# New figures, an overlap, tie numbers and four rules in the planner of a metaformer layer on one core

## The chip, the cores and the metric

The kernel runs on one core of one Trainium2 chip. The metric is the device time of one execution in microseconds (us). Before the change it is 3187.56 us, the median of 3 runs (3181.11 to 3189.2).

## What is computed

One metaformer layer on x of shape (8, 384, 32, 32), all in float32: 8 images b, each 1024 tokens of 384 channels. First comes a selective state-space block with its own MLP, then a feed-forward block with sign-binarised weights and group-wise 8-bit quantisation. Cut to what matters:

```python
# block 1, tokens t = layernorm(x)
xz = t @ in_proj_w.T;  xm, z = split(xz)                  # 768 channels each
xc = silu(causal_conv3(xm))
dt, Bm, Cm = split(xc @ x_proj_w.T)                       # 24, 16, 16
dt = softplus(dt @ dt_proj_w.T + dt_proj_b)
h[l] = exp(dt[l] * A) * h[l-1] + (dt * xc)[l] * Bm[l]     # 16 states a channel, 1024 steps
y = (sum over states of h * Cm + xc * D) * silu(z)
x = x + gelu((y @ out_proj_w.T) @ mlp_w1.T + b1) @ mlp_w2.T + b2
# block 2, images 0 to 4 alone get a quantised branch that is not zero
h = quant(layernorm(x) @ sign(W1 - mean).T + b1)
x = x + quant(gelu(h) @ sign(W2 - mean).T + b2)
```

Quantisation needs the largest absolute value of a whole image, twice per image.

## The kernel before, in words

All work of the eight images is written down once as a list of operations and then put in order by a planner that runs while the program is built. `Layer.write_down` (L1286 on) goes through the images: `s1` (L654: norm, input projections, convolution, dt), `s2` and `scan` (L813, L826: the recurrence), `s3` (L1001: output projection and MLP) and, for images 0 to 4, `ffn` (the quantised block). Each `Plan.add` (L212) records an engine, a cost in us, a function that issues the instruction, and the tiles it reads and writes. From the tiles the planner derives which operation waits for which.

`Plan.run` (L258) is a list scheduler. It keeps a clock for each engine (`free`), takes the engine that can start first, lets `choose` (L281) pick one of the operations that can start at that moment (`able`, those whose start is not after `now`), issues it, and advances the engine's clock by the cost. So the costs decide the order of the instructions on each engine and nothing else; each engine then executes its list in that order. The parts that matter here:

- Engines. TensorE (PE) does all matrix products, and the sums over states of the scan (`py`, L907). GpSimd (POOL) does the products with B and C (`u`, `dtx_r`, L942). VectorE (DVE) does the scans (L967), a part of the C products (L987, L989), convolution taps and some copies out of PSUM. ScalarE (ACT) does the exponentials `da` (L556), the silu, softplus and gelu functions (L556 as well) and most copies out of PSUM (L569, L571). SP issues nearly all transfers.
- Choice on ACT. exp, silu, softplus and gelu need different function tables; a change costs an ACT_TABLE_LOAD (planner's price `LOAD_TABLE` 1.29). `choose` stays in the loaded table while such an operation can start (`same`, except exp), else takes an exp or an operation without a table (`plain`), and changes to another table only when neither can start.
- Groups of functions. `in_place` (L670) and `gelu` apply a function to three pieces of 128x1024. The first piece reads all parts of the group (`r=parts if p == 0`), and the second and third overwrite parts the first has read; so they depend on the first, and their `ready` time is its end (L378 on, with no signal added, since the engine is the same).
- Choice on DVE and POOL. Operations of the stages (`prio[0] > 0`) go before those of the scan (`prio[0] == 0`).
- Ties. `rank` (L295) orders by lane, image and age. In each 100 us of planned time, a number from `TURNS` scrambles the age by up to 16 places (`turned`, L96).
- Fillers. Where the planner sees PE idle for more than `IDLE` 0.7 us, it puts matmuls of a constant there (`spare`, 128x256, L443 to L454), to hold the TensorE clock up. They do no part of the computation.
- Buffers: two PSUM tiles for `da`, three for products (`mm`), one for `py`; three `u` and two `dtx_r` in SBUF, nine `hid` for the hidden layer.
- The end. After the last `py` come the last products of the last half image in a row: `p_out`, 36 `p_h`, 36 `p_o` and the last store.

Of the kernel before, what the change touches and what calls it, by code (L numbers as in the profile page):

```python
# [71 lines left out]
MM = 0.86  # L72
SWITCH = 0.26
BATCH = 2
# [12 lines left out]

STRETCH, REACH = 100, 16
TURNS = (
# [3 lines left out]
)  # L93


def turned(n, by):  # L96
# [3 lines left out]
    return (x ^ x >> 13) % (2 * REACH + 1) - REACH  # L100


def c_act(n):
    return 0.25 + n * 0.00084


def c_dve(n):
    return 0.19 + n * 0.00102


def c_pair(n):
    return 0.19 + n * 0.00188


def c_pool(n):
    return 0.18 + n * 0.00214

# [81 lines left out]
class Plan:  # L199
# [12 lines left out]
    def add(self, engine, cost, emit, r=(), w=(), claim=(), table=None, size=0, others=None,  # L212
            land=1.6):
        op = Op()
        op.engine, op.cost, op.emit, op.table = engine, cost, emit, table
        op.others, op.settle = others or {}, None
        op.size, op.land, op.prio = size, land, (*self.prio, len(self.ops))
        op.next, op.ready, op.tiles = [], 0.0, []
        op.slack = SLACK if self.prio[0] < 0 else 0.0
        deps = set()  # L220

        def parts_of(t):
            t, part = t if isinstance(t, tuple) else (t, None)
            if t not in op.tiles:
                op.tiles.append(t)
                if t.ring is not None:
                    t.left += 1
            if part is None:
                if None not in t.parts:
                    t.parts[None] = [None, []]  # L230
                return list(t.parts.values())
            if part not in t.parts:
                whole = t.parts.get(None)
                t.parts[part] = [whole[0], list(whole[1])] if whole else [None, []]
            return [t.parts[part]]

        for t in claim:
            t.left += 1
            op.tiles.append(t)
        for t in r:  # L240
            for p in parts_of(t):
                if p[0] is not None:
                    deps.add(p[0])
                p[1].append(op)
        for t in w:
            for p in parts_of(t):
                if p[0] is not None:
                    deps.add(p[0])
                deps.update(p[1])
                p[0], p[1] = op, []  # L250
        deps.discard(op)
        op.wants = len(deps)
        for d in deps:
            d.next.append(op)
        self.ops.append(op)
        return op

    def run(self):  # L258
# [22 lines left out]
        def choose(e, now, able):  # L281
            able = [op for s, op in able if s <= now]
            if e == "ACT":
                same = [op for op in able if op.table == table and table != "exp"]
                plain = [op for op in able if op.table in (None, "exp")]
                able = same if table is not None and same else plain or able
            if e in ("DVE", "POOL"):

                able = [op for op in able if op.prio[0] > 0 and op.ready <= now - PATIENCE] or [
                    op for op in able if op.prio[0] == 0] or able  # L290
            at = int(now / STRETCH)
            turn = TURNS[at] if at < len(TURNS) else 0
            return min(able, key=lambda op: rank(op, turn))

        def rank(op, turn):  # L295


            lane, b = op.prio[:2]
            if lane <= 0:
                first = (lane, b)  # L300
            elif lane == 7:
                first = (EARLY, b)
            elif lane in (1, 4, 11, 14):
                first = (1, b) if b <= max(scanned + 1, FRONTS) else (3, b)
            else:
                first = (2, b)
            return (*first, op.prio[2] + (turned(op.prio[2], turn) if turn else 0))

# [12 lines left out]
        while left:  # L321
# [45 lines left out]
            if op.table is not None and op.table != table:  # L367
                cost += LOAD_TABLE
                table = op.table
            end = free[e] = clock.run(now, cost) if e == "PE" else now + cost  # L370
            if e == "SP":
                dma_free = max(dma_free, end + 0.5) + 0.05 + op.size / 360e3
                end = dma_free + op.land
# [17 lines left out]
class Layer:  # L391
# [115 lines left out]

    def load(self, to, view, src, r=(), size=0, cost=0.46, land=2.3):

        self.plan.add(  # L510
            "SP", cost, lambda: self.nc.sync.dma_start(view(to.real), src), r=r, w=[to],
            size=size, land=land,
        )
# [8 lines left out]
    def rows_moved(self, t, parts, move, r, w):  # L522
        n = P // len(parts)
        for i, mem in enumerate(parts):
            self.plan.add(
                "SP", 0.42, lambda i=i, mem=mem: move(t.real[i * n : (i + 1) * n, :], mem),
                r=r, w=w(i), size=4 * n * T,
            )

    def weights(self, ring, k, src, r=()):  # L530
        w = self.piece(ring, [P, k, P], ring)
        self.load(w, lambda t: t, src, r=r, size=4 * P * k * P, cost=0.37, land=1.5)
        return w
# [28 lines left out]
    def affine(self, out, in_, r, w, bias=0.0, scale=1.0, n=T, pool=False):  # L562
# [19 lines left out]
        if pool:  # L582
            others = {"POOL": (0.18 + n * 0.00095, on(nc.gpsimd))}
        else:
            others = {"DVE": (c_dve(n), on(nc.vector))}
        extra = 0.0 if plain else 0.09 if isinstance(scale, float) else 0.18
        self.plan.add("ACT", 0.16 + n * 0.00083 + extra, on_act, r=r, w=w, others=others)

    def norm(self, t, eps, scale):

        nc, add = self.nc, self.plan.add
        def columns(src, name):
# [10 lines left out]

            add("PE", 0.9, emit, r=[src], w=[p])
            return p

        def spread(src, name, turned=False):
# [29 lines left out]
        p_turned = self.piece("mm", [P, G], "p_turned")  # L637
        add("PE", 0.5, lambda: nc.tensor.matmul(
            p_turned.real, var.real, self.ident[:, ::DQ], start=True, stop=True
# [3 lines left out]
            r=[p_turned], w=[rstd])  # L643
        add("POOL", 0.8, lambda: nc.gpsimd.tensor_tensor(
            rstd.real, rstd.real, self.power.to_broadcast([P, G]), ALU.pow
# [8 lines left out]
    def s1(self, b):  # L654
# [46 lines left out]
        for half, cols in enumerate(HALVES):  # L701
# [4 lines left out]
            for m in range(KD):  # L706
# [12 lines left out]
                for s in (1, 2):  # L719
                    add("DVE", c_dve(T) + 0.06, lambda m=m, xc=xc, pm=pm, s=s, tap=tap: (  # L720
                        nc.vector.scalar_tensor_tensor(
# [4 lines left out]
            if half:  # L726
# [6 lines left out]

                add("POOL", 0.9, edge, r=[halo[m] for m in range(KD)], w=[self.edged])
                for p, piece in enumerate(xc.pieces):
                    add("POOL", 0.25, lambda p=p, piece=piece: nc.gpsimd.tensor_add(
                        piece.real[:, :, :2], piece.real[:, :, :2],
# [19 lines left out]

            add("PE", 0.26 + KC * MM, low, r=[w, *all_m], w=[p_dbc], claim=[dbc])
            self.affine(lambda dbc=dbc: dbc.real, lambda p_dbc=p_dbc: p_dbc.real, [p_dbc], [dbc])
# [66 lines left out]
    def scan(self, b, half, state):  # L826
# [7 lines left out]

        def load(to, view, src, r, size):
            self.plan.add("SP", 0.57, lambda: nc.sync.dma_start(view(), src), r=r, w=[to],  # L836
                          size=size, land=2.3)

        def quad_rows(i):
            r = self.piece(f"bc{i}", [P, n], f"bc{i}")  # L840
            src = rows.real[i * SQ : (i + 1) * SQ, cols].unsqueeze(0).to_broadcast([DQ, SQ, n])
            load(r, lambda: r.real, src, [rows[h] for h in halves], 4 * P * n)
            return r
# [90 lines left out]
    def scan_pair(self, u, cols, n, dts, dtxs, bq, cq, state, half, on_pool):  # L934
# [14 lines left out]
        for t, mine in enumerate(cols):  # L949
            da = self.piece("da", [P, wide, n], "da")  # L950
            dt_r = dts[t]
            for i, col in enumerate(mine):
                self.act(
                    lambda i=i, da=da: da.real[:, i, :],
                    lambda i=i, dt_r=dt_r: dt_r.real[:, i, :], AF.Exp,
                    0.26 + n * 0.00084, r=[dt_r[i]], w=[da], table="exp",
                    scale=self.a_neg[:, col : col + 1],
# [43 lines left out]
    def s3(self, b):  # L1001
        nc, a, add = self.nc, self.a, self.plan.add
        yg_d = self.dram["yg", b]
        for half, cols in enumerate(HALVES):
# [12 lines left out]
            else:  # L1017
                yg = self.split("hid", KD, "yg")
                for p, piece in enumerate(yg.pieces):
# [5 lines left out]
                        w=[piece[k] for k in range(PER)], claim=yg.pieces[p:],  # L1025
                        size=4 * P * PER * T, land=2.3,
                    )
# [21 lines left out]
            for m in range(KC):  # L1049
                rows = slice(m * P, (m + 1) * P)  # L1050
                res = self.piece("res", [P, T], "res")

                self.load(res, lambda t: t, a["x"][b, rows, cols], r=[g[HK]], size=4 * P * T)
                po = self.mlp_out(lambda i, m=m: a["mlp_w2"][m, i], "w6", g, [res], "p_o")
# [145 lines left out]
    def clip(self, view, n, parts, q):  # L1200
        self.plan.add("POOL", 0.13 + n * 0.0009, lambda: self.nc.gpsimd.tensor_scalar(
            view(), view(), q.real[:, 2:3], q.real[:, 1:2], ALU.min, ALU.max
        ), r=[q], w=parts)

    def ffn(self, b):
# [32 lines left out]
        for h, cols in enumerate(HALVES):  # L1238
            g = self.split("hid", KH, "gf")
            for p, piece in enumerate(g.pieces):  # L1240
# [3 lines left out]
                    r=[y1_d[h, p * PER + m] for m in range(PER)], w=parts,  # L1244
                    claim=g.pieces[p:], size=4 * P * PER * T, land=2.3)
                self.clip(lambda piece=piece: piece.real, PER * T, parts, q1)
# [135 lines left out]
```

## Time and profile before

| What | Value |
|---|---|
| Median of 3 runs | 3187.56 us |
| Profiled execution | 3184.62 us, its span 3182.5 us, mean TensorE clock 0.988 |
| Instructions in the trace | 33759 |
| Matmul records | 10972, two for each float32 matmul |
| Mean DMA rate | 236 GB/s, 751.85 MB |

An engine's busy time is the union of its instructions' times. A matmul of the program leaves two records, so a record count is twice the number of matmuls. Idle time of an engine is put down to what ended it ("<- ACT da L556" is an activation that writes `da`). The chain that ended last starts at 2928.10 us and is made mostly of PE in its last 100 us.

### The profile page before, as it was taken

The page shows a single profiled execution, that of the slowest core. Times are in us where ns is not written, and L with a number is a line of the kernel's source. Part 1 is how long each engine was busy: PE and PEld are TensorE (multiplying, and loading weights), DVE is VectorE, ACT ScalarE, POOL GpSimd, SP SyncE. Part 2 cuts the span into 40 slices and gives each one's busy share as a digit, 9 for nine tenths or more (in the row PEclk, how much of TensorE's full clock was granted, in tenths as well). Part 3 has the DMA queues.
Part 4 walks back from the last instruction along what each step waited for, and adds up shares of the span by engine and source line. Part 5 has one row for each costly group of instructions (what it writes and reads, how often), then busy time and mean ns, then how long its engine had stood idle before and what let it go on. Part 6 is the DMA issues. An engine that isn't in the chain of part 4 may idle for free. (4 is left out here: it accounts for less than half of the span.)

```text
span 3182.5 us, 33759 instructions
## 1 busy us (share of the span) xinstructions
PE 3083.4 (97%) x10972; PEld 1274.9 (40%) x10972; DVE 2644.0 (83%) x2081; ACT 1966.5 (62%) x2363; POOL 2744.8 (86%) x1046
## 2 busy tenths in 40 slices
PE   9898999999999999999999999999999999999999
PEld 4333434343433443433444434343434443433334
DVE  4697888899788798879998888889789987888881
ACT  4777786855665556665656655666566555655552
POOL 1788889988988978999979999799989999998980
PEclk9998999999989999999999999999999999999999
DMA  7797789757786667875696766877677856756542
GB/s 231 261 310 263 252 261 329 255 195 259 239 283 221 198 227 254 295 250 185 230 319 234 252 207 232 298 236 254 219 257 254 282 196 213 235 175 209 160 148 72
DMA packets 348975, 751.85 MB, mean 236 GB/s; under 512 B 36481, under 2 KB 113793, under 8 KB 339585
## 3 DMA queue, kind: packets, MB, share of 16 engines
q1 hardware_dynamic: 348368, 749.61, 71.0%
q8 instruction: 88, 1.44, 0.2%
q14 instruction: 87, 0.70, 0.1%
q10 hardware_dynamic: 432, 0.09, 0.0%
HBM read 569.21 MB, written 180.36 MB: 236 GB/s over the span
## 5 line engine op out<-in xcount | busy, mean ns | idle before, releaser
L942 POOL TENSOR_TENSOR u<-dtx_r,bc 128x2048 f32<-128x2048 f32 (+1 forms) x360 | 1185.5, 3308 | 124.9 <-PE py L907 79.7
L556 ACT ACTIVATE da<-dt_r,a_neg 128x1024 f32<-128x1024 f32 (+1 forms) x960 | 900.5, 945 | 490.0 <-DVE u L967 272.3
L942 POOL TENSOR_TENSOR u<-u,bc 128x2048 f32<-128x2048 f32 (+1 forms) x274 | 900.1, 3290 | 86.9 <-DVE u L967 81.4
L967 DVE TENSOR_TENSOR_SCAN u<-da,u 128x1024 f32<-128x1024 f32 (+1 forms) x436 | 869.1, 2007 | 127.1 <-POOL u L942 71.4
L540 PE MATMUL p_h<-t,w_b 128*128 128x512 f32 x1152 | 511.7, 597 | 10.8 <-DMA w_b<-in_mlp_w 6.8
L540 PE MATMUL p_o<-g,w 128*128 128x512 f32 x1152 | 512.6, 597 | 5.1 <-DMA w<-in_mlp_w 5.1
L967 DVE TENSOR_TENSOR_SCAN da<-da,dtx_r 128x1024 f32<-128x1024 f32 (+1 forms) x192 | 386.3, 2019 | 55.6 <-POOL dtx_r L942 34.2
L942 POOL TENSOR_TENSOR dtx_r<-dtx_r,bc 128x2048 f32<-128x2048 f32 (+1 forms) x120 | 396.8, 3311 | 2.4
L540 PEld LDWEIGHTS p_h<-t,w_b 128*128 128x128 f32 x1152 | 214.0, 190 | 298.0 <-issue 257.7
L540 PEld LDWEIGHTS p_o<-g,w 128*128 128x128 f32 x1152 | 214.3, 190 | 295.8 <-issue 277.9
L540 PE MATMUL p_y<-tn,w_b 128*128 128x512 f32 x720 | 319.6, 597 | 2.2 <-DVE tn L648 2.2
L540 PE MATMUL p_y<-gf,w_n 128*128 128x512 f32 x720 | 320.3, 597 | 0.8 <-ACT gf L556 0.5
L907 PE MATMUL py<-u,fold 128*32 128x512 f32 x2304 | 303.5, 628 | 0.2 <-POOL u L942 0.2
L967 DVE TENSOR_TENSOR_SCAN da<-da,u 128x1024 f32<-128x1024 f32 (+1 forms) x140 | 283.7, 2041 | 13.7 <-POOL u L942 6.9
L540 PE MATMUL p_out<-yg,w 128*128 128x512 f32 x552 | 245.6, 597 | 4.2 <-DMA w<-in_out_proj_last 1.5
L540 PE MATMUL p_z<-t,w_f 128*128 128x512 f32 x504 | 233.4, 610 | 9.2 <-DMA w_f<-in_in_proj_w 5.1
L540 PE MATMUL p_in<-t,w_f 128*128 128x512 f32 x504 | 229.7, 601 | 5.6 <-DMA w_f<-in_in_proj_w 3.7
L556 ACT ACT_TABLE_LOAD x172 | 220.7, 1283 | 3.1
L540 PEld LDWEIGHTS p_y<-gf,w_n 128*128 128x128 f32 x720 | 133.9, 190 | 185.3 <-issue 173.8
L540 PEld LDWEIGHTS p_y<-tn,w_b 128*128 128x128 f32 x720 | 134.0, 190 | 182.1 <-issue 165.1
L571 ACT ACTIVATE g<-p_h,v_vecs 128x512 f32<-128x512 f32 x158 | 107.7, 684 | 145.2 <-PE p_h L540 144.7
L571 ACT ACTIVATE y<-p_y,v_vecs 128x512 f32<-128x512 f32 x138 | 94.2, 684 | 166.9 <-PE p_y L540 139.0
(132 smaller groups left out, 3245.0 us busy)
## 6 DMA issues: line engine op xcount, KB each, us to landing
dt_r<-dt_d SPq DMA_DIRECT2D x144, 512.0 KB, 5.5
dtx_r<-dtx_d SPq DMA_DIRECT2D x72, 1024.0 KB, 6.0
w_b<-in_mlp_w SPq DMA_DIRECT2D x192, 192.0 KB, 3.1
w<-in_mlp_w SPq DMA_DIRECT2D x96, 384.0 KB, 3.5
w_f<-in_in_proj_w SPq DMA_DIRECT2D x168, 192.0 KB, 4.8
y_d<-y SPq DMA_DIRECT2D x120, 256.0 KB, 4.7
gf<-y_d SPq DMA_DIRECT2D x60, 512.0 KB, 6.9
xc_d<-xc SPq DMA_DIRECT2D x48, 512.0 KB, 5.6
```

The costliest lines, as they stand in the source:

```text
L540: self.nc.tensor.matmul(p.real, w.real[:, w0 + k, :], t.at(k0 + k), start=start and k == 0, stop=stop and k == n - 1,)
L556: lambda: self.nc.scalar.activation(out(), in_(), func, **{k: v() if callable(v) else v for k, v in kw.items()}),
L571: nc.scalar.activation(out(), in_(), AF.Identity, bias=bias, scale=scale)
L907: nc.tensor.matmul(py.real[g * DQ : (g + 1) * DQ, :], self.fold, hc, start=False, stop=(q == NQUAD - 1), skip_group_check=True,)
L942: nc.gpsimd.tensor_mul(u.real[:, x], t.real[:, x], row.real.unsqueeze(2).to_broadcast([P, n, 2]))
L967: da=da, in_u=in_u: nc.vector.tensor_tensor_scan(to(i), da.real[:, i, :], in_u(i), state.real[:, col : col + 1] if half else 0.0, ALU.mult ...
```

## The change

No operation of the computation is added or removed, and no buffer changes; what changes is what the planner believes and how it chooses.

1. Overlap (`LAG`): the planner's clock of ACT runs free 0.09 us before the operation's end, that of DVE 0.08 us before.
2. Figures: base costs of ACT, DVE and POOL operations, of several PE operations, and the rates and landing times of transfers. A transfer now occupies the planned DMA queue for 0.03 us plus its size by its own rate, and every landing gets 0.2 us more.
3. A new table `TURNS` of 29 numbers for 100 us each. Its lower 16 bits are the tie number as before. Four bits above switch rules on in that stretch: `LATE_FRONTS` (the front stage of a next image ranks behind the other stages), `DVE_SCANS` and `POOL_SCANS` (the scan goes before the stages on that engine), `ACT_STAGES` (among operations of ACT without another table, those of the stages go first). `LATE_FRONTS` stands in 7 stretches, `DVE_SCANS` in 5, `POOL_SCANS` in 6, `ACT_STAGES` in 6.

The diff, without lines that change one figure of the same kind:

```diff
-SWITCH = 0.26
+SWITCH = 0.22
...
+LATE_FRONTS, DVE_SCANS, POOL_SCANS, ACT_STAGES = 1 << 16, 1 << 17, 1 << 18, 1 << 19
 TURNS = (
-    19522, 59978, 49910, 0, 34827, 0, 6565, 14275, 0, 7565, 33371, 19911,
-    57895, 25116, 28986, 13399, 22123, 50761, 24784, 16788, 35300, 27386, 48162, 5457,
-    0, 0, 40719, 11435, 20253, 0, 2806, 25936,
+    55348, 285972, 34779, 0, 32856, 50975, 5477, 811041, 712524, 58073,
+    309902, 321043, 90863, 34708, 35186, 643484, 561450, 159751, 20316, 55659,
+    17295, 33505, 202442, 110152, 635446, 91750, 507399, 59652, 924931,
 )
...
+LAG = {"ACT": 0.09, "DVE": 0.08}
...
 def c_act(n):
-    return 0.25 + n * 0.00084
+    return 0.2 + n * 0.00084
 def c_dve(n):
-    return 0.19 + n * 0.00102
+    return 0.17 + n * 0.00102
 def c_pair(n):
-    return 0.19 + n * 0.00188
+    return 0.22 + n * 0.00188
...
     def add(self, engine, cost, emit, r=(), w=(), claim=(), table=None, size=0, others=None,
-            land=1.6):
+            land=1.6, rate=350e3):
...
-        op.size, op.land, op.prio = size, land, (*self.prio, len(self.ops))
+        op.size, op.land, op.prio = 0.03 + size / rate, land + 0.2, (*self.prio, len(self.ops))
...
         def choose(e, now, able):
             able = [op for s, op in able if s <= now]
+            at = int(now / STRETCH)
+            turn = TURNS[at] if at < len(TURNS) else 0
             if e == "ACT":
                 same = [op for op in able if op.table == table and table != "exp"]
                 plain = [op for op in able if op.table in (None, "exp")]
                 able = same if table is not None and same else plain or able
+                if turn & ACT_STAGES:
+                    able = [op for op in able if op.prio[0] > 0 and op.table in (None, "exp")] or able
             if e in ("DVE", "POOL"):
-                able = [op for op in able if op.prio[0] > 0 and op.ready <= now - PATIENCE] or [
-                    op for op in able if op.prio[0] == 0] or able
-            at = int(now / STRETCH)
-            turn = TURNS[at] if at < len(TURNS) else 0
+                scans = [op for op in able if op.prio[0] == 0]
+                if not (turn & (DVE_SCANS if e == "DVE" else POOL_SCANS) and scans):
+                    able = [op for op in able if (
+                        op.prio[0] > 0 and op.ready <= now - PATIENCE)] or scans or able
+                else:
+                    able = scans
...
             elif lane in (1, 4, 11, 14):
-                first = (1, b) if b <= max(scanned + 1, FRONTS) else (3, b)
+                soon = 2.5 if turn & LATE_FRONTS else 1
+                first = (soon, b) if b <= max(scanned + 1, FRONTS) else (3, b)
...
-            return (*first, op.prio[2] + (turned(op.prio[2], turn) if turn else 0))
+            by = turn & 0xFFFF
+            return (*first, op.prio[2] + (turned(op.prio[2], by) if by else 0))
...
-            end = free[e] = clock.run(now, cost) if e == "PE" else now + cost
+            end = clock.run(now, cost) if e == "PE" else now + cost
+            free[e] = end - LAG.get(e, 0.0)
             if e == "SP":
-                dma_free = max(dma_free, end + 0.5) + 0.05 + op.size / 360e3
+                dma_free = max(dma_free, end + 0.4) + op.size
                 end = dma_free + op.land
...
-    def load(self, to, view, src, r=(), size=0, cost=0.46, land=2.3):
+    def load(self, to, view, src, r=(), size=0, cost=0.46, land=2.0, rate=350e3):
...
-        self.load(w, lambda t: t, src, r=r, size=4 * P * k * P, cost=0.37, land=1.5)
+        self.load(w, lambda t: t, src, r=r, size=4 * P * k * P, cost=0.36, land=1.5,
+                  rate=350e3 if k > KC else 440e3)
...
-            add("PE", 0.9, emit, r=[src], w=[p])
+            add("PE", 0.78, emit, r=[src], w=[p])
...
-            add("PE", 0.26 + KC * MM, low, r=[w, *all_m], w=[p_dbc], claim=[dbc])
+            add("PE", 0.15 + KC * MM, low, r=[w, *all_m], w=[p_dbc], claim=[dbc])
...
-        def load(to, view, src, r, size):
+        def load(to, view, src, r, size, land=1.8, rate=320e3):
             self.plan.add("SP", 0.57, lambda: nc.sync.dma_start(view(), src), r=r, w=[to],
-                          size=size, land=2.3)
+                          size=size + 80e3, land=land, rate=rate)
```

More of the change, by code (lines that the diff above doesn't have):

```diff
@@ L100, in turned @@
     return (x ^ x >> 13) % (2 * REACH + 1) - REACH
+LAG = {"ACT": 0.09, "DVE": 0.08}
 def c_act(n):
-    return 0.25 + n * 0.00084
+    return 0.2 + n * 0.00084
 def c_dve(n):
-    return 0.19 + n * 0.00102
+    return 0.17 + n * 0.00102
 def c_pair(n):
-    return 0.19 + n * 0.00188
+    return 0.22 + n * 0.00188
 def c_pool(n):
-    return 0.18 + n * 0.00214
+    return 0.19 + n * 0.00214
 class Clock:
@@ L505, in constants @@
         nc.vector.tensor_scalar_mul(self.a_neg, self.a_neg, -1.0)
-    def load(self, to, view, src, r=(), size=0, cost=0.46, land=2.3):
+    def load(self, to, view, src, r=(), size=0, cost=0.46, land=2.0, rate=350e3):
         self.plan.add(
             "SP", cost, lambda: self.nc.sync.dma_start(view(to.real), src), r=r, w=[to],
-            size=size, land=land,
+            size=size, land=land, rate=rate,
         )
@@ L526, in rows_moved @@
                 "SP", 0.42, lambda i=i, mem=mem: move(t.real[i * n : (i + 1) * n, :], mem),
-                r=r, w=w(i), size=4 * n * T,
+                r=r, w=w(i), size=4 * n * T, land=1.6,
             )
@@ L584, in affine @@
         else:
-            others = {"DVE": (c_dve(n), on(nc.vector))}
+            others = {"DVE": (c_dve(n) + (0 if isinstance(scale, float) else 0.15), on(nc.vector))}
         extra = 0.0 if plain else 0.09 if isinstance(scale, float) else 0.18
@@ L637, in norm @@
         p_turned = self.piece("mm", [P, G], "p_turned")
-        add("PE", 0.5, lambda: nc.tensor.matmul(
+        add("PE", 0.3, lambda: nc.tensor.matmul(
             p_turned.real, var.real, self.ident[:, ::DQ], start=True, stop=True
@@ L643, in norm @@
             r=[p_turned], w=[rstd])
-        add("POOL", 0.8, lambda: nc.gpsimd.tensor_tensor(
+        add("POOL", 1.0, lambda: nc.gpsimd.tensor_tensor(
             rstd.real, rstd.real, self.power.to_broadcast([P, G]), ALU.pow
@@ L719, in s1 @@
                 for s in (1, 2):
-                    add("DVE", c_dve(T) + 0.06, lambda m=m, xc=xc, pm=pm, s=s, tap=tap: (
+                    add("DVE", c_dve(T) + 0.05, lambda m=m, xc=xc, pm=pm, s=s, tap=tap: (
                         nc.vector.scalar_tensor_tensor(
@@ L732, in edge @@
                     nc.gpsimd.tensor_add(e[:, :, :1], e[:, :, :1], one)
-                add("POOL", 0.9, edge, r=[halo[m] for m in range(KD)], w=[self.edged])
+                add("POOL", 0.65, edge, r=[halo[m] for m in range(KD)], w=[self.edged])
                 for p, piece in enumerate(xc.pieces):
-                    add("POOL", 0.25, lambda p=p, piece=piece: nc.gpsimd.tensor_add(
+                    add("POOL", 0.18, lambda p=p, piece=piece: nc.gpsimd.tensor_add(
                         piece.real[:, :, :2], piece.real[:, :, :2],
@@ L841, in quad_rows @@
             src = rows.real[i * SQ : (i + 1) * SQ, cols].unsqueeze(0).to_broadcast([DQ, SQ, n])
-            load(r, lambda: r.real, src, [rows[h] for h in halves], 4 * P * n)
+            load(r, lambda: r.real, src, [rows[h] for h in halves], 4 * P * n, 2.2, 440e3)
             return r
@@ L955, in scan_pair @@
                     lambda i=i, dt_r=dt_r: dt_r.real[:, i, :], AF.Exp,
-                    0.26 + n * 0.00084, r=[dt_r[i]], w=[da], table="exp",
+                    0.25 + n * 0.00084, r=[dt_r[i]], w=[da], table="exp",
                     scale=self.a_neg[:, col : col + 1],
@@ L1025, in s3 @@
                         w=[piece[k] for k in range(PER)], claim=yg.pieces[p:],
-                        size=4 * P * PER * T, land=2.3,
+                        size=4 * P * PER * T, land=2.0,
                     )
@@ L1051, in s3 @@
                 res = self.piece("res", [P, T], "res")
-                self.load(res, lambda t: t, a["x"][b, rows, cols], r=[g[HK]], size=4 * P * T)
+                self.load(res, lambda t: t, a["x"][b, rows, cols], r=[g[HK]], size=4 * P * T, land=2.3)
                 po = self.mlp_out(lambda i, m=m: a["mlp_w2"][m, i], "w6", g, [res], "p_o")
@@ L1200, in clip @@
     def clip(self, view, n, parts, q):
-        self.plan.add("POOL", 0.13 + n * 0.0009, lambda: self.nc.gpsimd.tensor_scalar(
+        self.plan.add("POOL", 0.2 + n * 0.00096, lambda: self.nc.gpsimd.tensor_scalar(
             view(), view(), q.real[:, 2:3], q.real[:, 1:2], ALU.min, ALU.max
@@ L1244, in ffn @@
                     r=[y1_d[h, p * PER + m] for m in range(PER)], w=parts,
-                    claim=g.pieces[p:], size=4 * P * PER * T, land=2.3)
+                    claim=g.pieces[p:], size=4 * P * PER * T, land=2.0)
                 self.clip(lambda piece=piece: piece.real, PER * T, parts, q1)
```

## The prediction, on record before the changed kernel ran

> **What bounds the kernel now.** I read the page's busy times first, then the stretches, the chain of waits, the groups and TensorE's waits.
>
> ```profile
> span 3182.5 us, 33759 instructions
> ...
> PE 3083.4 (97%) x10972; PEld 1274.9 (40%) x10972; DVE 2644.0 (83%) x2081; ACT 1966.5 (62%) x2363; POOL 2744.8 (86%) x1046
> ```
>
> PE is the engine to account for, POOL is the next, ACT has 1216 us free. But busy is not useful. Below are stretches of the span (start:end, length, then busy time by engine, then the granted clock):
>
> ```profile
> 75.00:400.00 325.00, 283.42 (x1096) 116.39 (x1095) 262.32 (x269) 244.37 (x355) 275.66 (x175) 0.93 0.82 272
> 400.00:2500.00 2100.00, 2066.69 (x7448) 848.32 (x7447) 1833.35 (x1343) 1321.11 (x1485) 1902.52 (x604) 0.99 0.74 249
> 2500.00:2700.00 200.00, 198.58 (x646) 86.66 (x645) 166.99 (x124) 114.69 (x120) 191.33 (x63) 1.00 0.66 222
> 2700.00:3113.00 413.00, 400.50 (x1252) 158.29 (x1250) 345.67 (x294) 233.94 (x332) 367.98 (x191) 1.00 0.58 180
> ```
>
> PE idles 41.6 us of the 325 early ones, at a reduced clock, and 33.3 of the next 2100. From 2500 to 2700 it looks full; the same stretches asked for `spare` alone give 17.76 us of that to fillers. The chain gives the step of PE:
>
> ```profile
> 3050.93 1.94 PE py L907 x16
> ...
> 3116.57 0.43 PE spare L451 x2
> 3117.00 30.90 PE p_h L540 x72
> 3147.90 30.91 PE p_o L540 x72
> ```
>
> A record of a large product takes 30.90/72 = 0.4292 us, a record of py 1.94/16 = 0.1213, a filler (two records) 0.43. The last py comes at 3113, and 66 us of PE work that nothing can overlap follow: these stay.
>
> **Useful work of PE.** From the record counts of the groups: p_o 1152, p_h 1152, p_y 1440, p_out 576, p_z 576, p_in 576 are 5472 x 0.4292 = 2348.4 us; py 3072 x 0.1213 = 372.5; the small products (norms, dt, dbc, sums) have 262.0 us of busy time in their rows. Sum 2982.9. The span less that is 199.6 us: fillers 114 x 0.43 = 49.0, and 150.6 of idle time, half speed and drains. (Idle on the page is 3182.5 - 3083.4 = 99.1.)
>
> ```profile
> PE p_sums L1122 <- DMA w<-in_W: 6.8, 2, 3.9
> PE p_h L540 <- DMA w_b<-in_mlp_w: 6.8, 6, 1.8
> PE p_o L540 <- DMA w<-in_mlp_w: 5.1, 4, 2.3
> PE p_z L540 <- DMA w_f<-in_in_proj_w: 5.1, 4, 3.5
> PE p_all L762 <- DVE mean L1146: 4.4, 1, 4.4
> ```
>
> No single wait rules: the longest names are weights and small results that came some us after the place that the planner had given their reader.
>
> **What the Trainium skill says.** "ScalarE: Activation LUTs", section What ACT_TABLE_LOAD costs: a load takes about 1283 ns and a drain of about 1380 more, and back-to-back activations overlap by about 93 ns. Trace, ACT in order of time:
>
> ```profile
> 1510.72 1.28 ACT L556 ACT_TABLE_LOAD   x1
> 1512.02 2.95 ACT L556 ACTIVATE g<-g 128x1024 f32<-128x1024 f32 x3
> ...
> 1515.57 1.28 ACT L556 ACT_TABLE_LOAD   x1
> 1516.86 2.15 ACT L556 ACTIVATE da<-dt_r,a_neg 128x1024 f32<-128x1024 f32 x2
> ```
>
> The load agrees (group mean 1283). The drain doesn't show: the idle time before all 172 loads is 3.1 us. I use 1.283. The overlap agrees: three gelus of mean 1047 ns cover 2.95, not 3.14, so 0.095 each. So `LAG` describes something real. "TensorE: Matmul & The Clock Gate", section What's actually happening: the clock falls to half after an idle window of about 3.4 us. The trace agrees, PE in order of time:
>
> ```profile
> 44.25 2.79 PE L752 MATMUL p_dbc<-xc,w_f 128*64 128x512 f32 x12
> ```
>
> ```profile
> 224.90 5.28 PE L752 MATMUL p_dbc<-xc,w_b 128*64 128x512 f32 x12 [3.69 <-ACT halo L569]
> ```
>
> The same product costs 2.5 us more after 3.69 us of idling. The same page, section Architectural detail, says that ACT and DVE are strict first-in first-out; no run here tests it, but it is why a misplaced operation holds up all behind it.
>
> **The change part by part.**
>
> *Fillers.* In the changed program as built there are 61 instead of 114. Ordered by the useful PE work ahead of them, they fall from 53 to 35 in the first 430 us of it, and from 40 to 3 between 2200 and 2400 (in time, the stretch from 2500 to 2700). 53 x 0.43 = 22.8 us less. Where PE would idle there instead, this gain is nil; both ends: 0 to -22.8. I take -22.8, since behind the fillers of 2500 to 2700 only 1.4 us of idling is left, so PE had work to go on with.
>
> *Figures, ties, the rules for DVE, POOL and fronts.* No duration changes, nor do the number of transfers (2255 SP instructions in both) or of matmuls other than fillers; all queues, SP's and POOL's included, are reordered from the start. The interleaving by and large stays: at the py that end the eight images' scans PE has done 438, 787, 1141, 1490, 1845, 2193, 2539, 2866 us of useful work, against 426, 782, 1136, 1490, 1845, 2197, 2529, 2866; the first py stands after 88 instead of 94. So what can move is the 150.6 us of misplacement. At best all of it goes, at worst it grows; the trace of before can't show which. Of the waits, 31.8 us are on transfers, whose figures were redone, and the rest is mostly on copies by ACT and DVE, whose figures were too long by just the overlap. I take a quarter, -37.7 us: somewhat more than the waits on transfers with no half-speed windows counted. This is a choice; the ends are -88 (POOL, below) and, taken as the fillers' gain lost again with the split tables' price, +32.
>
> *Table loads.* These come as a by-product of `LAG`. The second piece of a group becomes ready at the first one's end, and ACT now chooses 0.09 us before that; an exp that can start wins, and the table is changed back and forth. The built program shows it: ACT loads 256 instead of 173; function groups of exactly 3 fall from 78 to 39, and 42 stand as 1 before 2. 83 x 1.283 = 106.5 us more on ACT: 1966.5 to 2073, 65% of the span. The cover is the 490.0 us that ACT idles before `da`, mostly waiting for DVE to free a buffer. So I cost it at nothing. Against it: a torn group's last two pieces come 2 x 1.283 + 0.945 = 3.5 us later, 42 x 3.5 = 147 us, and PE's p_o or the next stage wait behind them. For it: a whole group keeps exp away for 5.5 us where DVE has two `da` tiles, about 4 us of scans (2.0 each) in hand; DVE waits 62.4 + 26.6 = 89.0 us for `da`, and a torn group shortens that. DVE doesn't set the end, so I take nothing for it.
>
> *Copies moved.* 16 copies of p_h go from ACT (684 ns) to DVE (744), other kinds by 1 to 5: 12 us on DVE, with over 500 idle. Nothing, or 12 if DVE were full. `LAG` on DVE likewise slips another operation between a scan and its product: at most one scan, 2.0 us, behind which py waits; hidden by the py's place, after many p_o.
>
> Sum: 3184.6 (span 3182.5 and 2.1 around it) - 22.8 - 37.7 = 3124.1. The median shown lies 3.0 above the profiled run: 3127.
>
> **Rivals.**
>
> *Only the planned part comes:* other misplacements replace the old. 3184.6 - 22.8 + 3 = 3165. For it: idle time is spread over some 50 kinds of waits. Against: the figures were moved toward what the trace shows.
>
> *POOL becomes the bound.* POOL has 2744.8 - 7.3 (first 75 us) = 2737.4 us to do between 75 and 3113, and idles 300.6. PE causes 79.7 (u <- py) and 30.8 (dtx <- p_var) of that; the other 190 stays. Then 75 + 2737.4 + 190 + 69.5 + 2.1 + 3 = 3077 is the end of what PE can gain. For it: 86% busy. Against: it needs nearly 110 of PE's 199.6 us to go.
>
> *Nothing comes of it:* 16% of the 147 us of torn groups reaches PE, 23 us, as much as the fillers bring: 3187.
>
> *Slower, by the torn groups.* Place: PE at p_o (and p_y, x_proj, dt stores) behind the second and third piece. If 35% of the 147 us reaches PE: +51.5 - 22.8 = +28.7, so 3216. It decides from (22.8 + 9.6)/147 = 22% on. For it: PE is in order and 97% busy, and ACT's order is fixed. Against: nine `hid` tiles let products of other stages stand between.
>
> **Numbers.** 0.3% of 3187 is 9.6 us, about what a measurement can tell from no change. Likeliest 3127, chance 0.44; planned part alone 0.17; POOL's bound 0.14; nothing 0.09; slower 0.16. Faster 0.75, same 0.09, slower 0.16. The range, 3068 to 3198, leaves out most of the slower case and a little below POOL's bound, some 0.18.
>
> **What would show it.** Right: `spare` x122 and 26 us; PE's idle time and the 0.93 clock of 75 to 400 better; ACT_TABLE_LOAD near x255 and 328 us while ACT's idling before `da` shrinks; last py about 3055. Wrong: p_o or py waiting for `g`, `dt` or `xc` pieces with tens of us; more half-speed windows; POOL without idle time.

## The result, and the profile after

The changed kernel takes 3166.86 us (median of 4 runs, 3165.13 to 3170.19) against 3188.38 us (4 runs, 3181.11 to 3193.61): a ratio of 0.9935, 95% interval 0.9914 to 0.9957, 21 us less. The forecast was 3127. So the gain is about a third of the 61 us that were forecast. The time lies in the range, near its rival "only the planned part comes" (3165); that rival's mechanism turns out to be wrong all the same.

The page after: span, then busy time of each engine.

```profile
span 3163.5 us, 33667 instructions
...
PE 3071.7 (97%) x10866; PEld 1259.6 (40%) x10866; DVE 2620.7 (83%) x2091; ACT 2060.3 (65%) x2432; POOL 2749.1 (87%) x1050
```

The span is 19.0 us shorter. ACT works 93.8 us more, and PE 11.7 less. The same stretches as before, the last one ending at the last py, 19 us earlier:

```profile
75.00:400.00 325.00, 293.15 (x1113) 117.45 (x1111) 263.08 (x271) 265.96 (x382) 278.90 (x178) 0.94 0.86 290
400.00:2500.00 2100.00, 2069.21 (x7452) 850.83 (x7453) 1830.55 (x1368) 1372.65 (x1512) 1914.44 (x603) 0.99 0.74 247
2500.00:2700.00 200.00, 198.48 (x606) 78.09 (x608) 168.89 (x119) 129.55 (x131) 194.64 (x67) 0.98 0.69 225
2700.00:3094.00 394.00, 377.96 (x1186) 149.13 (x1176) 326.31 (x286) 240.54 (x336) 351.42 (x187) 1.00 0.58 181
```

PE idles 31.9 us from 75 to 400 (41.6 before) and 30.8 up to 2500 (33.3), but 16.0 instead of 12.5 in the last stretch. The groups of the table loads and the fillers, before and after, as forecast in number (PE rows show two records for each filler):

```profile
L556 ACT ACT_TABLE_LOAD x172 | 220.7, 1283 | 3.1
...
L451 PE MATMUL spare<-small 128*128 128x256 f32 x228 | 58.1, 394 | 0.0
```

```profile
L569 ACT ACT_TABLE_LOAD x255 | 327.2, 1283 | 4.6
...
L463 PE MATMUL spare<-small 128*128 128x256 f32 x122 | 37.4, 418 | 0.8 <-ACT dt L584 0.7
```

A torn function group, ACT in order of time: one gelu, the table changed back for two exponentials, and again for the other two gelus.

```profile
1480.81 1.28 ACT L569 ACT_TABLE_LOAD   x1
1482.11 1.06 ACT L569 ACTIVATE g<-g 128x1024 f32<-128x1024 f32 x1
1483.18 1.28 ACT L569 ACT_TABLE_LOAD   x1
1484.48 2.16 ACT L569 ACTIVATE da<-dt_r,a_neg 128x1024 f32<-128x1024 f32 x2
1486.65 1.28 ACT L569 ACT_TABLE_LOAD   x1
1487.95 2.00 ACT L569 ACTIVATE g<-g 128x1024 f32<-128x1024 f32 x2
...
1490.55 1.28 ACT L569 ACT_TABLE_LOAD   x1
```

The longest waits of PE are again transfers of weights; the others are again short and of many kinds:

```profile
PE p_o L553 <- DMA w<-in_mlp_w: 8.6, 6, 2.6
PE p_h L553 <- DMA w_b<-in_mlp_w: 6.0, 5, 1.6
```

So by the profile alone, 53 fillers fewer (22.8 us) and 19 us less look like one and the same thing. The first experiments were made to test that.

### The profile page after: what moved, and what is told of

It reads as the page before. It is cut to its first block, busy times and chain, and to the rows that moved or that the text cites. A ratio compares the mean times of both kernels' runs of the same rounds, so it can differ in the third digit from the quotient of the medians.

```text
span 3163.5 us, 33667 instructions
## 1 busy us (share of the span) xinstructions
PE 3071.7 (97%) x10866; PEld 1259.6 (40%) x10866; DVE 2620.7 (83%) x2091; ACT 2060.3 (65%) x2432; POOL 2749.1 (87%) x1050
## 4 chain that ended last, share of the span: by engine, by line
PE 64%; DVE 12%; ACT 11%; POOL 5%; issue 4%; DMA 3%; SPq 0%; DVEq 0%; POOLq 0%; ACTq 0%
PE p_y L553 17%; PE p_h L553 11%; PE p_o L553 10%; PE py L920 8%; PE p_out L553 6%; PE p_z L553 5%; DVE da L980 4%; DVE u L980 4%; POOL u L955 4%; PE p_in L553 4%; ACT L569 3%; ACT da L569 3%; PE p_dt L796 1%; DMA dtx_r<-dtx_d 1%; ACT g L569 1%
## 5 line engine op out<-in xcount | busy, mean ns | idle before, releaser
L569 ACT ACTIVATE da<-dt_r,a_neg 128x1024 f32<-128x1024 f32 (+1 forms) x960 | 895.5, 944 | 487.5 <-DVE u L980 292.9
L569 ACT ACT_TABLE_LOAD x255 | 327.2, 1283 | 4.6
L584 ACT ACTIVATE y<-p_y,v_vecs 128x512 f32<-128x512 f32 x141 | 96.1, 682 | 123.7 <-PE p_y L553 102.8
L584 ACT ACTIVATE g<-p_h,v_vecs 128x512 f32<-128x512 f32 x142 | 96.3, 681 | 115.6 <-PE p_h L553 115.1
```

Of the source, the lines that this page charges most:

```text
L569: lambda: self.nc.scalar.activation(out(), in_(), func, **{k: v() if callable(v) else v for k, v in kw.items()}),
L584: nc.scalar.activation(out(), in_(), AF.Identity, bias=bias, scale=scale)
```

## The experiments

All ratios are against the kernel before, run on the same chip in the same job; 1% of it is 32 us.

### Fillers

```diff
                     self.spare.real = ring.make(self.spare.shape, self.spare.name)
-                    self.fill()
                     free[e] = clock.run(free[e], MM / 2)
```

In the kernel before and in the changed one; the plan is the same, only the filler isn't issued.

> The kernel before with its plan kept and its 114 filler matmuls not issued; nothing of the computation is left out. Theory 1, a filler is plain TensorE time in place: 114 x 0.43 = 49 us go, less some 10 us because the first 18 fillers stand in the norms' waits and hold the clock up, so 3145 to 3150 us. Theory 2, the fillers stand in waits that are there without them and hold the clock up: 3185 us or more, and a lower granted clock before 400 us and from 2500 to 2700 us.

> The changed kernel with its plan kept and its 61 filler matmuls not issued; nothing of the computation is left out. Theory 1, fillers are plain TensorE time and their number is all that the change is worth: 61 x 0.43 = 26 us less some 10 for the first 14, so 3147 to 3152 us, and the same as the kernel before without fillers. Theory 2, the fillers cost nothing and the new order is what gained 19 us: about 3167 us, and some 20 us less than the kernel before without fillers.

Measured: before without fillers 1.0003 (0.9991 to 1.0015), after without fillers 0.9924 (0.9905 to 0.9942), to be held against 0.9935 with them. Theory 2 in both: the fillers cost nothing, and the gain is there without them (0.9924 against 1.0003, 25 us). What replaces them shows in two stretches of the kernel before without fillers:

```profile
75.00:400.00 325.00, 276.05 (x1030) 107.15 (x1029) 261.52 (x268) 244.20 (x355) 274.00 (x174) 0.91 0.83 272
2500.00:2700.00 200.00, 186.49 (x565) 72.61 (x564) 166.03 (x124) 114.31 (x120) 190.93 (x62) 0.97 0.69 229
```

From 2500 to 2700 PE now idles 13.5 us instead of 1.4 and the clock drops to 0.97; before 400 it is 0.91 instead of 0.93 (mean over the span 0.983 instead of 0.988). PE in order of time, same kernel:

```profile
2555.28 0.49 PE L1183 MATMUL p_max<-diag,small 128*128 128x128 f32 x2 [3.06 <-ACT diag L555]
2557.64 3.85 PE L906 MATMUL py<-u,fold 128*32 128x512 f32 x16 [1.88 <-POOL u L941]
...
2604.53 1.63 PE L906 MATMUL py<-u,fold 128*32 128x512 f32 x8 [2.21 <-POOL u L941]
```

Waits for ACT and POOL stand where the fillers stood. Over the whole span PE idles 133.5 us instead of 99.1, and its other products are busy for 3053.5 us instead of about 3034 (3083.4 less 114 x 0.43). So by this estimate the 49 us of fillers come back as some 34 us of waits and, at the lower clock, some 19 us of slower products.

### Table loads

Joined after the fact: in the changed kernel the plan is kept, but the first piece of a group issues the whole group.

```diff
+    def join_group(self, n):
+        ops = self.plan.ops[-n:]
+        emits = [op.emit for op in ops]
...
+        ops[0].emit = whole
+        for op in ops[1:]:
+            op.emit = lambda: None
```

`whole` calls all of `emits`.

> The changed kernel with its plan kept, but the second and third piece of each silu, softplus and gelu group issued right behind the first: the order of ScalarE alone changes, and its table loads fall from 256 to 180 in the program. Theory 1, the torn groups cost nothing, since ScalarE idles nearly 490 us before da: 3162 to 3172 us, no change. Theory 2, the torn groups ate the 38 us that the forecast took for better figures: faster by 20 to 40 us, 3127 to 3147. Theory 3, a torn group helps, since the exponentials come sooner: slower by 10 us or more, with more waiting of VectorE for da.

Measured 1.0045 (1.0027 to 1.0062): slower than the changed kernel by 1.0045/0.9935 - 1 = 1.1%, 35 us, with ACT 98.3 us less busy (1962.0 against 2060.3). This is theory 3, with its sign and its longer waits of VectorE for da: 112.7 us in the changed kernel (first fence), 138.3 in the joined one (second).

```profile
DVE u L980 <- ACT da L569: 83.9, 68, 3.4
...
DVE da L980 <- ACT da L569: 28.8, 23, 3.6
```

```profile
DVE u L993 <- ACT da L569: 93.8, 56, 5.4
...
DVE da L993 <- ACT da L569: 44.5, 24, 4.5
```

But the other engines still run a plan made for torn groups. So this run can't tell whether torn groups help, or whether any departure of ScalarE from the plan costs time; the planner with whole groups, further below, is for that.

Loads added to the kernel before, with its plan kept, by one line behind the first piece of every second group:

```diff
+            self.nc.scalar.activation(self.torn, self.one, AF.Exp)
```

> The kernel before with its plan kept, and behind the first piece of every second function group an exponential of one column into a tile that nobody reads: 100 more table loads (273 against 173), 50 x (2 x 1.283 + 0.2) = 138 us more on ScalarE, no other order changed. Theory 1, ScalarE's idle time covers them: 3186 to 3194 us. Theory 2, they reach TensorE with the 16% to 35% of the rivals in the forecast: 22 to 48 us more, 3210 to 3236.

Measured 1.0188 (1.0167 to 1.0209), 60 us for the 138 that were added: even above theory 2. VectorE waits 180.3 us for da instead of 89.0 (before, then with the added loads):

```profile
DVE u L967 <- ACT da L556: 62.4, 47, 5.8
...
DVE da L967 <- ACT da L556: 26.6, 22, 6.7
```

```profile
DVE u L984 <- ACT da L557: 135.4, 61, 8.8
...
DVE da L984 <- ACT da L557: 44.9, 22, 9.7
```

ACT's idle time before da didn't cover this; it even grew from 490.0 to 537.5 us, most of it ended by DVE:

```profile
L556 ACT ACTIVATE da<-dt_r,a_neg 128x1024 f32<-128x1024 f32 (+1 forms) x960 | 900.5, 945 | 490.0 <-DVE u L967 272.3
```

```profile
L557 ACT ACTIVATE da<-dt_r,a_neg 128x1024 f32<-128x1024 f32 (+1 forms) x960 | 900.7, 945 | 537.5 <-DVE u L984 289.8
```

In this time ACT waits for DVE to free one of the two `da` buffers. The likely reading is that a delayed exponential delays DVE, and DVE then frees the buffer later, so the idle time comes after the delay and not instead of it. How the delay goes on to PE is not shown: PE idles 140.4 us instead of 99.1, in many short waits of which none grew by more than 6 us, and it is busy 26 us longer at a mean clock of 0.983 instead of 0.988.

Loads taken away from both:

```diff
-            in_place(xc, AF.Silu, "silu")
+            in_place(xc, AF.Relu, "silu")
...
-            in_place(dt, AF.Softplus, "softplus")
+            in_place(dt, AF.Abs, "softplus")
...
```

> The kernel before with its plan kept and silu and gelu replaced by relu, softplus by the absolute value, which need no table of their own: the functions of the computation are left out, and 172 of 173 table loads with them, 221 us less on ScalarE. Theory 1, ScalarE's delays reach the end with 0.4 to 0.5 of their length, as the added loads did (63 of 138 us): 85 to 110 us faster, 3080 to 3105. Theory 2, only delays against the plan count, and ScalarE ahead of its plan gains little: 0 to 30 us faster, 3158 to 3188.

> The changed kernel with its plan kept and the same replacement of silu, gelu and softplus: those functions are left out, and 255 of 256 table loads, 327 us less on ScalarE. Theory 1, the 83 additional loads of the changed kernel cost time where they stand: it gains more from this than the kernel before does, by 83 x 1.283 x 0.45 = 48 us, so 3020 to 3040. Theory 2, the loads are covered by other work: a gain of 0 to 30 us, 3137 to 3167, no more than the kernel before gains.

Measured: before without loads 0.9989 (0.9979 to 0.9998), 3.5 us of 221 on ACT; after without loads 0.9867 (0.9825 to 0.9908), against 0.9935 with them a difference of 0.0068, 22 us of 327. In size this is theory 2 in both: an ACT that runs ahead of the plan brings little, though one that falls behind costs much. Against theory 2, the changed kernel gained more than the one before, by some 18 us. The intervals leave 3 to 33 for it (half widths of 0.0021 and 0.0041 added as squares); they are wide because the four runs of the changed kernel without loads lie in two pairs, 3136 and 3138, 3153 and 3158 us. Without loads the two orders differ by 0.9867/0.9989 = 0.9878, 39 us (25 to 52).

The page of the changed kernel without loads:

```profile
PE 3053.8 (97%) x10866; PEld 1255.9 (40%) x10866; DVE 2620.2 (84%) x2091; ACT 1726.6 (55%) x2177; POOL 2749.1 (88%) x1050
```

With ACT at 55% PE is still 97% full, with the same number of products. Against the changed kernel it idles 80.9 us instead of 91.8 and is busy 17.9 us less, at a mean clock of 0.991 in this profile instead of 0.987.

### Empty tables, and tables of equal effort

```diff
-TURNS = (
...
-)
+TURNS = ()
```

> The kernel before with an empty table of tie numbers: the planner's old figures, no overlap, ties by age. Its plan puts in 192 fillers. Theory 1, the gain of 21 us comes from the figures and the overlap, which place operations better whatever the ties: this kernel is some 20 us slower than the changed one with an empty table. Theory 2, the gain comes from the table alone: the two kernels with empty tables lie within 10 us of each other, both at 3210 to 3260, and what the table is worth is larger in the changed kernel by 21 us or more.

> The changed kernel with an empty table: new figures and overlap, ties by age, no rule on. Its plan puts in 184 fillers. Theory 1, figures and overlap are the gain: 20 us less than the kernel before with an empty table, about 3190 to 3220. Theory 2, the table is the gain: 3210 to 3260 and within 10 us of the kernel before with an empty table.

Measured: before 1.0203 (1.0176 to 1.023), after 1.0282 (1.0256 to 1.0309). Theory 1 has the sign wrong: with ties by age the new figures and the overlap are 0.8%, 25 us, slower, so the two are also further apart than the 10 us of theory 2. The table is worth 2.0% in the kernel before and 1.0282 - 0.9935 = 3.5% in the changed one; that the difference exceeds 21 us is as theory 2 had it.

Cleared rule bits, each number of the changed kernel's table cut to its lower 16 bits:

```diff
-    55348, 285972, 34779, 0, 32856, 50975, 5477, 811041, 712524, 58073,
+    55348, 23828, 34779, 0, 32856, 50975, 5477, 24609, 57164, 58073,
...
```

> The changed kernel with the rule bits of its table cleared and its tie numbers kept; from the second stretch on the plan is another one (203 fillers instead of 61). Theory 1, the table's worth is that of one whole plan found by search, and any edit of it falls back to the level of an empty table: 3260 to 3295. Theory 2, the tie numbers keep a part of their worth by themselves: 3190 to 3240.

Measured 1.0315 (1.029 to 1.0341): back at the level of an empty table, as theory 1 had it. The edit touches 15 of the 29 numbers, and two readings fit it. Either the numbers of a table hold only for the plan they were drawn for, since after a different decision in the second stretch the later ones meet another list of candidates; or the rules themselves carry the gain. The search without rules, below, speaks against the second.

For this reason the next runs compare planners at equal effort: for each stretch of 100 us in turn, 40 numbers were drawn and the one kept with which the plan ended first. First a planner with whole groups, with an empty table and with its own:

```diff
-                n.ready = max(n.ready, end + n.slack + (
+                n.ready = max(n.ready, (
+                    free[e] if n.engine == e == "ACT" and not n.others else end
+                ) + n.slack + (
```

> The changed kernel with an empty table and one more line in the planner: on ScalarE, what waits only for the operation before it on the same engine counts as ready when the engine is free, so function groups stay whole (173 table loads). Theory 1, the torn groups cost time also in a plan that knows of them: some 20 us less than the changed kernel with an empty table (3283), so 3250 to 3268, like the kernel before with an empty table. Theory 2, they help, as joining them afterwards suggested (+37 us): 3285 or more.

> As the last, with a table of its own, found by drawing 40 numbers for each stretch in turn (178 table loads). Theory 1, whole groups are the better base: 15 us or more below the torn kernel with a table of the same effort, about 3195 to 3230. Theory 2, torn groups help the scan: the same as that one or slower.

> The changed kernel's planner, groups torn, with a table found by the same 40 draws for each stretch (252 table loads): what a shorter search gives. Theory 1: 3215 to 3250, and 15 us or more above the whole kernel of the same effort. Theory 2: the same as that one or faster. Either way it should lie well above 3167, if the gain of the change is its table's.

> Whole groups with a table from 150 draws for each stretch (176 table loads). Theory 1, the table and whole groups add up: 3140 to 3170, at or below the changed kernel. Theory 2, torn groups are worth their loads: 3175 or more, above the changed kernel's 3167.

Then the old planner, and the new one without rules:

> The kernel before (old figures, no overlap, no rules) with a table found by 40 draws for each stretch, the effort of the torn kernel's 3216 us. Theory 1, the change's gain is search effort put into its table, and the new figures by themselves give no better plans: 3205 to 3235, not above the new planner's 3216 by more than 10 us. Theory 2, new figures and overlap let the same effort find better plans: 3230 or more.

> The changed kernel's planner with a table of tie numbers alone, no rule bit set, 40 draws for each stretch. Theory 1, the four rules are only more draws: within 10 us of the same effort with rules, 3206 to 3226. Theory 2, the rules open better orders: 3230 or more.

| Planner | Table | Loads | Ratio to before, 95% interval |
|---|---|---|---|
| old figures | the kernel before's | 173 | 1 |
| old figures | empty | 179 | 1.0203, 1.0176 to 1.023 |
| new, torn | empty | 281 | 1.0282, 1.0256 to 1.0309 |
| new, whole | empty | 173 | 1.0257, 1.0242 to 1.0272 |
| old figures | 40 draws | 175 | 1.0121, 1.0101 to 1.0142 |
| new, torn, with rules | 40 draws | 252 | 1.0082, 1.0056 to 1.0109 |
| new, torn, no rules | 40 draws | 263 | 1.0063, 1.0041 to 1.0085 |
| new, whole, with rules | 40 draws | 178 | 1.0043, 1.0026 to 1.0059 |
| new, whole, with rules | 150 draws | 176 | 0.999, 0.9979 to 1.0001 |
| new, torn, with rules | the change's | 256 | 0.9935, 0.9914 to 0.9957 |

What follows, with the reserve that each of these is one plan found by one search, and no search was repeated:

- The rules: no gain at equal effort. The time is 0.8% over the kernel before with them and 0.6% without, so theory 1 of that run.
- The new figures and the overlap: 0.8% slower with empty tables, but faster with searched ones. At 40 draws the new planner with rules is 0.4% ahead of the old one, with intervals that touch. Without rules, where nothing but figures and overlap differs, it is 0.6% ahead, 18 us (9 to 28), and the intervals are apart. The old planner's own run fell between its theories (3225.1 us; by the ratios 12 us above the new one with rules). So the figures by themselves don't help, but they may help a search, by nearly as much as the whole change gained.
- Whole groups: 0.25% and 0.4% better than torn ones in their own plans, with intervals that overlap. This agrees with the 18 us above, as a hint. At 40 draws the torn and the whole table came as theory 1 expected (3215.9 and 3199.1 us, 17 apart); with an empty table whole groups fell between the theories (3271.4).
- Effort: from 40 to 150 draws 0.5%, and from 40 draws to the change's own table 1.0082 - 0.9935 = 1.5%, 47 us. How many draws stand behind the change's table is not known. The 150 draws gave theory 2's number (3185.3 us, where it had 3175 or more), but no torn table of 150 draws was made, so this doesn't show that torn groups are worth their loads.

No version that computes the same is clearly faster than the changed kernel; the fillers can be left out of it for the same time.

## Why the prediction was right or wrong, point by point

- *"Useful work of PE"*, 2982.9 us, and a tail of PE work behind the last py: right. The last two rows of the chain take 30.90 and 30.91 us again, and the last py came at 3094, as far from the end as before. But the sum can't tell the terms apart. By it 3163.5 - 2982.9 = 180.6 us are left over, 26.2 of them fillers (61 x 0.43) and 154.4 the rest, against 49.0 and 150.6 before: as if the fillers had brought everything and the order nothing. The runs without fillers say otherwise.
- *"Fillers ... I take -22.8"*: this step failed. The measured term is nil, one of the two ends that the prediction itself named: leaving out all 114 changed the time by -3 to 5 us. The reason given failed too: "only 1.4 us of idling is left, so PE had work to go on with". Little idle time is left because a filler occupies the wait; without it 13.5 us appear. The fall from 114 to 61 was read from the built program and came true as a count. It tells that the planner expects less waiting, and isn't itself a saving.
- *"I take a quarter, -37.7 us"*: the two orders without loads are 39 us apart, but the prediction calls its quarter a choice, so the near number is luck. Its reason, figures closer to the trace, is neither shown nor refuted. With empty tables the new figures and the overlap made the time 25 us longer; with searched tables of equal effort they made it 12 us shorter with rules and 18 without. What is shown is that without a searched table there is no gain: the table is worth 3.5%, and clearing its rule bits lost all of that.
- *"Table loads ... I cost it at nothing"*: this step failed too. The count was right (255 in the trace, 327.2 us), the cover was not one. Taking the loads away brings 22 us in the changed kernel and 3.5 in the one before, so the loads of the changed kernel cost about 18 us more (3 to 33). That the 83 additional ones cost this is the nearest reading, not tested apart. With 39 off and 18 back the sum is -21; this restates the same four times and is no independent proof. The cover named, idling before da, was expected to shrink and stayed (487.5 us after 490.0); ACT idled less before its copies of p_h and p_y instead (115.6 and 123.7 us after 145.2 and 166.9, with 16 fewer copies of p_h on ACT). In the kernel before, added loads reached the end with 43% of their length while the idling before da grew. The slower rival, with 51.5 us for torn groups, had the right sign and too high a price. It looked for the delay in PE's waits for g, which are 3.1 us at p_o; DVE's waits for da grew from 89.0 to 112.7.
- *The first rival*, 3165, has the right number by chance: it kept the fillers' term, which is nil, and dropped the order's, which is the gain.
- *POOL's bound* was not reached: POOL idled 414 us of the span, still partly for py. *Copies moved* was not tested by itself; DVE got less busy, 2620.7 for 2644.0 us. These copies and the fillers show that the planner's costs decide more than the order: also which engine does a copy, and how many fillers there are.
- *"What would show it"*: fillers x122 and loads near x255 came, but the last py, at 3094 instead of 3055, was the line that said by how much the forecast was off.

So the forecast missed by two terms: it took 22.8 us for fillers that bring nothing, and nothing for loads that cost about 18. What stays open is where the gain of the order comes from: a better search, or the new figures and the overlap as that search uses them. A search as long as the change's was not made for the old figures, figures and overlap were not tried apart, and how much two searches of the same planner differ is not known.

## What to carry to other kernels

Filler and idle time of an engine that waits belong together: leaving out a filler shows the wait. So price it at nothing until the wait itself is shown to be gone. The idle time of an engine is not a cover by its length alone; ask what it waits for, and whether added work delays just that. Here ACT idled over a third of the time, and 60 of 138 added us reached the end. When an order comes from a search, compare changes of its model at equal search effort, and more than one search each if the differences are small. One edit of a tuned table can throw the whole plan back to an untuned one, here by 1.0315/0.9935, almost 4%.

## What the runs showed of the hardware that was not expected

- A table load costs its 1283 ns and nothing visible beside it: 255 loads have 4.6 us of idle time before them in all, and the next activation starts 0.02 us after.
- The 114 fillers held the granted clock only from 0.983 up to 0.988 of full speed, in the profiled runs, and the time was the same without them.
- With every engine's order fixed, ACT was one-sided in this kernel: 138 us more in its list cost 60 us, 221 us less gained 3.5.
